# A four-layer residual block: the last stores of First move to ScalarE's queue, and attention's first mask and gathers move one slot ahead

## The chip, the cores and the metric

The kernel runs on one core of one Trainium2 chip. A core has five engines with an instruction stream each: TensorE (PE), VectorE (DVE), ScalarE (ACT), GpSimd (POOL) and SyncE (SP). An engine works through its stream in order and waits on semaphores for the others. Transfers are issued from the streams of SP, ACT and POOL and are carried by 16 DMA engines. The metric is the device time of one execution in microseconds, as the median of several runs.

## The reference

`x` has 64 batches of 32 rows and 512 columns, in float32. Four layers are added to it in turn. All indices (which weight, which adapter, which pages, how long the cache is) are inputs.

```
x = x + L0(x)    W = weights[cond]                     (64, 32, 32);  einsum('bct,bcd->bdt', x, W)
x = x + L1(x)    x @ base.T + bias + (x @ A[id].T) @ B[id].T          adapters of rank 16
x = x + L2(x)    attention over a paged cache, 32 heads of queries, 8 of keys, D = 128:
                   q, k, v = x @ Wq.T, x @ Wk.T, x @ Wv.T
                   q, k = rope(rmsnorm(q)), rope(rmsnorm(k))          positions from cache_seqlens
                   keys = [k_cache[block_table] (512 rows), k (32 rows)], values alike
                   scores = q . keys / sqrt(D), cache rows >= cache_seqlens set to -1e30
                   out = (softmax(scores) . values) @ Wo.T
x = x + L3(x)    as L0, with other weights
```

## The kernel before, in words

The 2048 rows of x are 16 tiles of 128 rows (`NT`), four batches each. The kernel has two parts: one long scheduled part with L0, L1 and the attention of L2, and a last one with the product by Wo and L3.

**First** (class `First`, line 389) is L0 and L1 for one tile t: `load`, `fetch` (gathers of weights), `turn_x` and `keep_x` (PE multiplies x by the mix matrix so that it comes out turned, ACT copies it out of PSUM as `x1T`), `ranks` (PE, `h_ps`, from `x1T`), `linear` (PE, `l_ps`), `add` (DVE, writes the new x), `store_x`, `turn_out` (PE turns the new x), `keep_out` (ACT copies it out as `x2T`, the tile x_a or x_b), `store` (writes the turned rows to `xT_dram`), and for every second tile `sums` (DVE makes four half-tiles of sums and differences of a pair of tiles, in two tiles) and `store_sums` (writes these two tiles to `xS_dram`). The projections of attention read `xT_dram` and `xS_dram` later. `queue` (line 516) says who issues the three kinds of stores: SP up to tile 12, POOL for tiles 13, 14 and 15.

**Projections** (`Block`, `Norm`) run two tiles at a time, spread over 32 slots. A norm has `squares` (ACT, L720, four of them), `power` (POOL, L725 and L727: it makes `rstd`), and four pieces on DVE: `scale` (L732, needs `rstd`), `straight` (L739), `swapped` (L751) and `sum` (L761). `norm_piece` takes these four from one list, in order, as slots have room. Then PE turns the result (`turn`, L766) and ACT copies it out (`keep`, L778).

**Attention** (`Unit`, line 783) is one batch and half of the key heads: 128 units, each with four slots. A unit loads its keys by SP (`kT`, L804), gathers its values by POOL (`fetch_values`, L105, four gathers), makes its mask on POOL (`mask`, L819, tile `pen`), and in slot k of its four does the scores (PE, L848 and L851, into the one buffer `s_ps`), the masked reduction on DVE (L856, reads `pen` and frees `s_ps`) and the exponential on ACT (L867). Two slots later PE turns the probabilities (L890), three slots later it multiplies them by the values (L900).

**The order** is written out by hand. Time is counted in slots: 0 to 511 are the slots of attention, and negative ones come before it. `at(slot, where, do, ...)` puts a call on a plan, and `slot(i)` (line 1218) runs the plan of slot i in a fixed order: "fetch", "pool", then scores, values and turns of attention, then "out", "pe", "take", "late", "power", a norm piece, "turn", "dve", two norm pieces, "keep", "act", "store". The order in which calls are made is the order in each engine's stream. First's tile t has its home slot at -39 + 2t (line 1077): its `store_x` is in slot home + 3, `store` in home + 4 and `store_sums` in home + 5, all in "store"; `keep_out` is in home + 3 and `keep_x` in home, both in "keep"; `sums` is in home + 4, "power". So tile 15 (home -9) does `keep_x` in slot -9, `keep_out` and `store_x` in -6, `store` and `sums` in -5, and `store_sums` in -4; tile 13 (home -13) does `sums` in slot -9. The last norms before attention have their power steps in slots -5, -3 and -2. Their pieces on DVE follow: `scale` and `straight` of the norm with the power step of slot -3 are in slot -1, ahead of slot 0's masked reduction.

**Memory.** The tiles of First are in the pool `first`. When slot -2 begins, that pool is closed (line 1314), and the pools of attention (`pages`, `v`, `attn`, and `ps_o` in PSUM) are opened in the memory that it leaves. The first tile of a new pool waits for the last uses of the old one. The first unit's mask and its first two gathers are in "pool" of slot -2, its other two gathers in "pool" of slot -1.

Of the kernel before, what the change touches and what calls it, by code (L numbers as in the profile page):

```python
# [45 lines left out]
NT = B * S // P  # L46
# [6 lines left out]
KG = HK // NG  # L53
# [24 lines left out]
def resid_kernel(  # L78
# [19 lines left out]
    nc = tc.nc  # L98
# [109 lines left out]
    xT_dram = [dram.tile([P, NC, P], F32, name=f"xT_{t}") for t in range(NT)]  # L208

    xS_dram = [dram.tile([P, 2, NC, P], F32, name=f"xS_{p}") for p in range(NT // 2)]  # L210
# [16 lines left out]
    with ExitStack() as l2:  # L227
# [161 lines left out]
        class First:  # L389
# [123 lines left out]
                if p == 0:  # L513
                    pair_of[0].x["12"], pair_of[0].x["34"] = s, r

            def queue(self):

                return nc.sync if self.t < NT - 3 else nc.gpsimd

            def store_x(self):  # L520
                self.queue().dma_start(out=x_dram[self.t], in_=self.x)

            def store(self):
                self.queue().dma_start(out=xT_dram[self.t], in_=self.x2T)

            def store_sums(self):
                for i in (0, 1):
                    self.queue().dma_start(out=xS_dram[self.t // 2][:, i], in_=self.s[i])

        lora = {}  # L530
        last_scores = []
# [418 lines left out]
        def at(slot, where, do, *args):  # L950
            plan.setdefault((slot, where), []).append((do, args))
# [5 lines left out]
        step_of, pair_of, unit_of, turn_of, first_of = {}, {}, {}, {}, {}  # L957
# [118 lines left out]
        for t in range(NT):  # L1076
            home = -WINDOW - AHEAD - 6 + 2 * t
            f = [first_of, t]
            if t:
                at(home - 5 if t > 1 else begin, "fetch", make, *f, First, t)  # L1080
                at(home - 4 if t > 1 else begin + 1, "fetch", call, *f, "load")
            at(max(begin, home - 4) if t > 1 else begin, "pool", call, *f, "fetch")
            if t % 2 == 0:
                at(home - 3 if t else begin, "pool", call, *f, "fetch_a")
                if t == 0:
                    at(begin, "pool", call, *f, "fetch_b")
            at(home - 1, "power", call, *f, "diagonal")
            if t:
                for name in "ax"[t % 2 :]:
                    at(home, "turn", call, *f, f"turn_{name}")  # L1090
                    at(home, "keep", call, *f, f"keep_{name}")
                at(home + 1, "late", call, *f, "ranks")
                at(home + 1, "late", call, *f, "linear", (0, 1, 2))
            else:

                at(home, "turn", call, *f, "turn_x")
                at(home, "keep", call, *f, "keep_x")
                at(home, "act", call, turn_of, -1, "turn")
                at(home, "act", call, *f, "linear", (0, 1, 2, 3))
                at(home, "act", call, turn_of, -1, "keep")  # L1100
                at(home, "act", call, *f, "turn_a")
                at(home, "act", call, *f, "keep_a")
                at(home + 1, "late", call, *f, "ranks")
            at(home + 1, "power", call, *f, "own_ranks")
            at(home + 2, "pe", call, *f, "linear", (3, 4) if t else (4,))
            at(home + 2, "power", call, *f, "add")
            at(home + 3, "store", call, *f, "store_x")
            at(home + 3, "turn", call, *f, "turn_out")
            at(home + 3, "keep", call, *f, "keep_out")
            at(home + 4, "store", call, *f, "store")  # L1110
            if t % 2:
                at(home + 4, "power", call, *f, "sums")
                at(home + 5, "store", call, *f, "store_sums")

            home = SLOTS * t + 9
            turning.add(home)
            at(home - 6, "fetch", lambda t: make(turn_of, t, Turn, 1, t, room["pages"], 1), t)
            at(home, "turn", call, turn_of, t, "turn")
            at(home, "keep", call, turn_of, t, "keep")
            at(home + 1, "store", call, turn_of, t, "store")  # L1120
# [14 lines left out]
                at(-27 + c, "store", store_angles, c)  # L1135
        for u in range(len(units)):
            at(KG * (u - 1) if u > 1 else (ready, -1)[u], "fetch", make, unit_of, u, Unit, u)
            at(KG * (u - 1) + 1 if u else -2, "pool", call, unit_of, u, "mask")
            for c in range(NC):
                at(KG * u - 2 + c if u else -2 + c // 2, "pool", call, unit_of, u, "fetch_values")  # L1140
            at(u // NB * SLOTS + 4 + 3 * (u % NB), "fetch", call, unit_of, u, "fetch_new")
            at(KG * u - 2, "act", call, unit_of, u, "begin")

# [46 lines left out]
        home = n - 33  # L1190
# [72 lines left out]
        with tc.manual_schedule(engines=ENGINES):  # L1263

            lora["base"] = first_pool.tile([P, NC, HID], F32, name="base_sb")
            make(first_of, 0, First, 0)
            first_of[0].load()
            with_identity()
            adapt_sb = first_pool.tile([P, NT // 2], I32, name="adapt_sb")
            for i in (0, 1):  # L1270
                nc.sync.dma_start(
                    out=adapt_sb[i * P // 2 : (i + 1) * P // 2, :],
                    in_=bass.AP(
                        tensor=ints.tensor,
                        offset=ints.offset + I_ADAPT + i,
                        ap=[[2 * N_INT, P // 2], [2, NT // 2]],
                    ),
                )
            for half in (lo, hi):
                nc.sync.dma_start(out=lora["base"][:, half, :], in_=base_w[:, half, :])  # L1280
            lora["rows"] = rows_of(first_pool, "lora_rows", adapt_sb, NT // 2, RANK, lane16_f)

            lora["bias"] = first_pool.tile([P, HID], F32, name="bias_sb")
            slot(begin)
            more = angles()
            next(more)
            nc.gpsimd.dma_start(out=lora["bias"], in_=across(base_b, HID))
            for i in range(begin + 3, begin + 15):
                for _ in range(1 + (begin + 5 < i < begin + 11)):
                    at(i, "store", next, more, None)  # L1290
            for j in (0, 1):
                at(begin + 4, "store", load_kv_weights, 0, 1, j)
                at(begin + 5, "store", load_kv_weights, 0, 0, j)
            for c in range(2 * KG):
                at(begin + 8 + c, "store", load_q_weights, 0, c // 2, c % 2)
            for i in range(begin + 1, begin + 11):
                slot(i)
                if i == begin + 2:
                    for c in range(NC):
                        base_chunk(c)  # L1300
                    lora["mask"] = [own_ranks(0), own_ranks(1)]
                    nc.sync.dma_start(out=table, in_=ints[:, I_TABLE:])
                if i == begin + 8:
                    nc.vector.tensor_copy(seq_f, ints_sb[:, I_SEQ : I_SEQ + B])
                    key_i = wpool.tile([P, LA], I32, name="key_i", tag="w9")
                    nc.gpsimd.iota(key_i, pattern=[[1, LA]], base=0, channel_multiplier=0)
                    nc.vector.tensor_copy(key_f, key_i)
                    nc.vector.memset(key_f[:, L:], -BIG)
                    v_rows = rows_of(const, "v_rows", table, B * NC, PSIZE, lane32_f)
            for i in range(begin + 11, n + VLAG):  # L1310
                if i == ready - 1:
                    start.close()
                    room["kT"] = l2.enter_context(tc.tile_pool(name="kT", bufs=2))
                if i == -2:
                    first.close()
                    pages = ExitStack()
                    room["pages"] = pages.enter_context(
                        tc.tile_pool(name="pages", bufs=1, side="right")
                    )
                    room["v"] = l2.enter_context(tc.tile_pool(name="v", bufs=2))  # L1320
                    room["attn"] = l2.enter_context(tc.tile_pool(name="attn", bufs=2))
                    room["o"] = l2.enter_context(tc.tile_pool(name="ps_o", bufs=1, space=PSUM))
                if i == SLOTS * NT + 8:
                    pages.close()
                if i == n - 27:
                    assert not pieces
                    proj.close()
                    o_pools.append(
                        ctx.enter_context(tc.tile_pool(name="o_first", bufs=1, side="right"))
                    )  # L1330
                slot(i)
            run(n + VLAG, "store")
# [205 lines left out]
```

## Time and profile before

| | us |
|---|---|
| median of 3 runs | 2435.49 |
| lowest and highest run | 2434.86, 2442.51 |
| the profiled execution | 2438.05 |
| its span, from the first instruction to the last | 2436.2 |
| PE busy between 200 and 250 us | 50.00 of 50.00 |
| PE busy between 166 and 172 us | 4.94 of 6.00 |
| PE busy between 174.0 and 178.9 us | 2.46 of 4.90 |
| mean TensorE clock granted over the span | 0.999 |
| mean clock between 179.9 and 181.5 us | 0.55 |
| mean clock between 181.5 and 183.5 us | 0.51 |

Times inside the profile count from the start of the span. In a row of the timeline the first number is the start, the second the duration, then come engine, line, operation, the tiles written and read, and in brackets the idle time of the engine before the row and what ended it. In the waits, a row gives the engine and line that waited, what it waited for, the total, the number of times and the longest. In the table of stretches, the columns after the stretch's own length are the busy times of PE, PE's weight loads, DVE, ACT and POOL with their counts of instructions, then the granted clock, the share of the DMA engines and GB/s. Slot 0 begins at 174.5 us, with the first scores.

### The profile page before, as it was taken

Reading aid. Unit: us, or ns where it says so; the run is one execution under the profiler, and the core shown is the slowest. Engines: PE = TensorE matmul, PEld = TensorE weight load, DVE = VectorE, ACT = ScalarE, POOL = GpSimd, SP = SyncE. Lnnn points to the kernel's source line nnn. Section 1 sums busy time; section 2 is a strip of 40 time slices with the busy share of each in tenths; the row PEclk is TensorE's granted clock in tenths of the full one; section 3 lists DMA queues with packets and bytes.
Section 4 is the critical chain, followed back from the end, with each engine's and each line's share of the span. In section 5 each row is a group of like instructions: output and inputs, shape, how many; then the busy total and the mean of one; then the engine's idle time right before and its main releaser. Section 6 shows DMA issues by size and latency. Waiting matters only on the chain.

```text
span 2436.2 us, 47122 instructions
## 1 busy us (share of the span) xinstructions
PE 2401.7 (99%) x13792; PEld 1865.9 (77%) x13792; DVE 1651.7 (68%) x3555; ACT 1401.0 (58%) x4006; POOL 1231.2 (51%) x1269
## 2 busy tenths in 40 slices
PE   8999999999999999999999999999999999999999
PEld 4657777777777777777777777777777788888887
DVE  6557777777777777787777777777787756333222
ACT  2346777777777777777777777767677763000000
POOL 4336665566565657665665666665556653000000
PEclk9999999999999999999999999999999999999999
DMA  8876666676666677766666666666667874333221
GB/s 277 258 240 181 196 191 205 184 207 184 204 184 203 191 213 242 231 187 189 179 185 176 190 176 184 180 186 182 180 181 226 251 250 143 107 119 122 87 90 59
DMA packets 461055, 452.09 MB, mean 186 GB/s; under 512 B 67728, under 2 KB 383760, under 8 KB 457216
## 3 DMA queue, kind: packets, MB, share of 16 engines
q1 hardware_dynamic: 404960, 269.05, 36.7%
q0 software_dynamic: 55024, 179.25, 24.7%
q8 instruction: 111, 1.82, 0.3%
q14 instruction: 144, 1.18, 0.2%
q10 hardware_dynamic: 816, 0.79, 0.1%
HBM read 380.73 MB, written 76.55 MB: 188 GB/s over the span
## 4 chain that ended last, share of the span: by engine, by line
PE 92%; DMA 3%; ACT 1%; DVE 1%; SPq 1%; issue 1%; POOL 0%; ACTq 0%; DVEq 0%; POOLq 0%
PE proj_ps L664 23%; PE o_ps L900 17%; PE out_ps L1362 15%; PE s_ps L848 10%; PE pT_ps L890 9%; PE s_ps L851 9%; PE head_ps L766 3%; PE l_ps L481 2%; PE o_ps L913 1%; DMA kT<-kT 1%; DMA o<-oT 1%; PE s_ps L883 1%; SPq L804 1%; PE mix_ps L1380 1%; PE x1T_ps L450 1%
## 5 line engine op out<-in xcount | busy, mean ns | idle before, releaser
L105 POOL DMA_INDIRECT v_sb<-v,v_rows x512 | 544.2, 1063 | 361.7 <-PE o_ps L900 248.3
L900 PE MATMUL o_ps<-pT,v_sb 128*128 128x128 f32 x4096 | 624.5, 275 | 2.9 <-DVE pT L892 2.6
L900 PEld LDWEIGHTS o_ps<-pT,v_sb 128*128 128x128 f32 x4096 | 578.0, 191 | 31.0 <-DVE pT L892 3.9
L867 ACT ACTIVATE sm<-sm,top 128x544 f32<-128x544 f32 x512 | 380.8, 744 | 335.2 <-DVE top L856 245.5
L856 DVE CUSTOM_DVE_ANT_0 sm<-s_ps,pen 128x544 f32<-128x544 f32 x512 | 369.3, 721 | 112.7 <-PE s_ps L851 97.1
L873 ACT ACTIVATE sm<-sm,share 128x512 f32<-128x512 f32 x512 | 369.8, 722 | 105.3 <-DVE share L872 68.5
L892 DVE COPY pT<-pT_ps 128x512 f32<-128x512 f32 x512 | 353.2, 690 | 60.2 <-PE pT_ps L890 12.5
L848 PE MATMUL s_ps<-kT,qT 128*128 128x288 f32 x1024 | 335.0, 409 | 3.3 <-DVE top L856 2.4
L890 PE MATMUL pT_ps<-ident,sm 128*128 128x128 f32 x2048 | 309.9, 274 | 4.3 <-ACT qT L778 3.7
L676 DVE TENSOR_TENSOR raw<-proj_ps,raw 128x512 f32<-128x512 f32 x332 | 224.3, 688 | 132.2 <-PE proj_ps L664 115.9
L851 PE MATMUL s_ps<-kT,qT 128*128 128x256 f32 x1024 | 304.8, 379 | 2.0 <-DMA kT<-kT 1.0
L848 PEld LDWEIGHTS s_ps<-kT,qT 128*128 128x128 f32 x1024 | 179.5, 191 | 151.0 <-issue 128.3
L819 POOL TENSOR_SCALAR pen<-key_f,seq_f 128x544 f32<-128x544 f32 x128 | 283.2, 2212 | 13.2 <-DMA kT<-kT 1.9
L890 PEld LDWEIGHTS pT_ps<-ident,sm 128*128 128x128 f32 x2048 | 239.1, 142 | 8.3 <-ACT qT L778 4.8
L720 ACT ACTIVATE sq<-raw 128x128 f32<-128x128 f32 x640 | 198.4, 310 | 73.9 <-DVE raw L676 56.0
L851 PEld LDWEIGHTS s_ps<-kT,qT 128*128 128x128 f32 x1024 | 194.6, 190 | 56.5 <-issue 1.4
L105 POOL DMA_INDIRECT mix_rows<-in_w,cond_rows x32 | 37.3, 1165 | 344.2 <-DVE mix_diag L170 299.8
L872 DVE RECIPROCAL share<-total 128x1 f32<-128x1 f32 x512 | 83.9, 164 | 180.4 <-ACT sm L867 153.1
L725 POOL TENSOR_SCALAR ss<-ss 128x4 f32<-128x4 f32 x160 | 38.6, 241 | 308.7 <-ACT sq L720 303.0
L1412 ACT COPY p<-out_ps 128x256 f32<-128x256 f32 x7 | 2.6, 372 | 333.1 <-PE out_ps L1362 333.1
L664 PE MATMUL proj_ps<-sum,x 128*128 128x512 f32 x380 | 188.0, 597 | 0.0
L727 POOL TENSOR_TENSOR rstd<-ss,minus_half 128x4 f32<-128x4 f32 x160 | 169.8, 1061 | 13.4
(175 smaller groups left out, 3573.7 us busy)
## 6 DMA issues: line engine op xcount, KB each, us to landing
kT<-kT SPq DMA_DIRECT2D x2048, 64.0 KB
o_in<-o SPq DMA_DIRECT2D x28, 1024.0 KB
o<-oT POOLq DMA_DIRECT2D x69, 256.0 KB
o<-oT SPq DMA_DIRECT2D x58, 256.0 KB
v<-in_kv_cache SPq DMA_DIRECT2D x32, 256.0 KB
kT<-page_rows SPq DMA_DIRECT2D x32, 256.0 KB
vn<-raw SPq DMA_DIRECT2D x32, 256.0 KB
v_sb<-v,v_rows POOLq DMA_INDIRECT x512
```

The lines of the kernel that those rows point to most:

```text
L105: nc.gpsimd.indirect_dma_start(out=dst, out_offset=None, in_=table, in_offset=bass.IndirectOffsetOnAxis(ap=index, axis=0),)
L664: nc.tensor.matmul(self.ps, lhsT=self.pair.x[x][:, c if x == "b" else half.start + c, :], rhs=blocks(self.b)[w][:, c, :], start=(c == 0), ...
L819: nc.gpsimd.tensor_scalar(self.pen, key_f, seq_f[:, self.b : self.b + 1], BIG, ALU.is_ge, ALU.mult)
L848: nc.tensor.matmul(ps[:, first:HID], lhsT=q, rhs=self.kT[:, :n1, k, :], start=True, stop=True)
L851: nc.tensor.matmul(ps[:, HID : first + LA], lhsT=q, rhs=self.kT[:, n1:, k, :], start=True, stop=True)
L856: nc.vector.tensor_tensor_reduce(out=sm, in0=ps[:, first : first + LA], in1=self.pen, scale=1.0, scalar=3e38, op0=ALU.add, op1=ALU.min, ac ...
L867: nc.scalar.activation(sm, sm, AF.Exp, bias=top, scale=-1.0, accum_out=total)
L873: nc.scalar.activation(sm[:, :L], sm[:, :L], AF.Copy, scale=share)
L890: nc.tensor.transpose(ps[:, c, :], self.sm[k][:, c * P : (c + 1) * P], ident)
L892: nc.vector.tensor_copy(pT, ps)
L900: nc.tensor.matmul(o_of[self.s, k][:, self.j, :], lhsT=self.v[c][:, k * D : (k + 1) * D], rhs=self.pT[k][:, c, :], start=(self.j == 0 and ...
L1362: nc.tensor.matmul(ps[:, :HALF], lhsT=o[:, i, :], rhs=w[i // REP][:, i % REP, :], start=(i == 0), stop=(i == KG * REP - 1),)
```

## The change

For tiles 13, 14 and 15, `store` and `store_sums` are issued by ACT instead of POOL; `store_x` stays on POOL. `store` of these tiles moves from "store" of slot home + 4 to "keep" of slot home + 3, right behind `keep_out`, and `store_sums` of tiles 13 and 15 from "store" of slot home + 5 to "turn" of slot home + 4, which comes after the DVE sums of the same slot. The pool `first` is closed and attention's pools are opened at slot -3 instead of -2; the first unit's mask and first two gathers are in "pool" of slot -3, the other two gathers in "pool" of slot -2.

```diff
-            def queue(self):
-
-                return nc.sync if self.t < NT - 3 else nc.gpsimd
+            def queue(self, last=nc.gpsimd):
+
+                return nc.sync if self.t < NT - 3 else last
 
             def store_x(self):
                 self.queue().dma_start(out=x_dram[self.t], in_=self.x)
 
             def store(self):
-                self.queue().dma_start(out=xT_dram[self.t], in_=self.x2T)
+                self.queue(nc.scalar).dma_start(out=xT_dram[self.t], in_=self.x2T)
 
             def store_sums(self):
                 for i in (0, 1):
-                    self.queue().dma_start(out=xS_dram[self.t // 2][:, i], in_=self.s[i])
+                    self.queue(nc.scalar).dma_start(out=xS_dram[self.t // 2][:, i], in_=self.s[i])
...
             at(home + 3, "store", call, *f, "store_x")
             at(home + 3, "turn", call, *f, "turn_out")
             at(home + 3, "keep", call, *f, "keep_out")
-            at(home + 4, "store", call, *f, "store")
+            at(home + 3 if t > NT - 4 else home + 4, "keep" if t > NT - 4 else "store", call, *f, "store")
             if t % 2:
                 at(home + 4, "power", call, *f, "sums")
-                at(home + 5, "store", call, *f, "store_sums")
+                if t > NT - 4:
+                    at(home + 4, "turn", call, *f, "store_sums")
+                else:
+                    at(home + 5, "store", call, *f, "store_sums")
...
-            at(KG * (u - 1) + 1 if u else -2, "pool", call, unit_of, u, "mask")
+            at(KG * (u - 1) + 1 if u else -3, "pool", call, unit_of, u, "mask")
             for c in range(NC):
-                at(KG * u - 2 + c if u else -2 + c // 2, "pool", call, unit_of, u, "fetch_values")
+                at(KG * u - 2 + c if u else -3 + c // 2, "pool", call, unit_of, u, "fetch_values")
...
-                if i == -2:
+                if i == -3:
                     first.close()
                     pages = ExitStack()
```

## The prediction

> **What bounds the kernel now.** I first read the busy times of the page, then PE's busy time by stretches of 50 us, then whom PE waited for.
>
> ```profile
> PE 2401.7 (99%) x13792; PEld 1865.9 (77%) x13792; DVE 1651.7 (68%) x3555; ACT 1401.0 (58%) x4006; POOL 1231.2 (51%) x1269
> ...
> 150.00:200.00 50.00, 44.75 (x188) 27.13 (x187) 31.82 (x70) 25.68 (x76) 27.60 (x33) 0.97 0.69 209
> 200.00:250.00 50.00, 50.00 (x311) 38.76 (x310) 38.35 (x84) 36.93 (x109) 30.88 (x32) 1.00 0.63 175
> ...
> PE s_ps L848 <- DVE top L856: 2.4, 1, 2.4
> ```
>
> TensorE sets the time: 2401.7 of 2436.2 us, so whatever happens can win only from 34.5 us of idle time. The stretch 150 to 200 us, where First ends and attention begins, holds 5.25 us of it; the next one holds none. So an engine other than PE matters only where PE waits for it, and that is at slots -9 to 1, the place of this change. PE's longest wait there is 2.4 us at slot 1's scores, for DVE's reduction of slot 0's. The timeline of POOL, then that of DVE, shows what is behind it.
>
> ```profile
> 165.12 0.54 POOL L521 DMA_DIRECT2D x<-x_sb  x1 [2.74 <-DVE x_sb L429]
> 169.30 0.23 POOL L725 TENSOR_SCALAR ss<-ss 128x4 f32<-128x4 f32 x1 [3.65 <-ACT sq L720]
> 169.61 1.05 POOL L727 TENSOR_TENSOR rstd<-ss,minus_half 128x4 f32<-128x4 f32 x1
> 170.64 0.63 POOL L524 DMA_DIRECT2D xT<-x_b  x1
> 171.26 1.08 POOL L528 DMA_DIRECT2D xS<-x  x2
> 172.42 0.48 POOL L725 TENSOR_SCALAR ss<-ss 128x4 f32<-128x4 f32 x1
> 172.98 1.07 POOL L727 TENSOR_TENSOR rstd<-ss,minus_half 128x4 f32<-128x4 f32 x1
> 175.95 2.12 POOL L819 TENSOR_SCALAR pen<-key_f,seq_f 128x544 f32<-128x544 f32 x1 [1.90 <-DMA kT<-kT]
> 178.36 1.11 POOL L105 DMA_INDIRECT v_sb<-v,v_rows  x1 [0.28 <-issue]
> 179.77 0.96 POOL L105 DMA_INDIRECT v_sb<-v,v_rows  x1 [0.30 <-issue]
> 180.81 0.58 POOL L725 TENSOR_SCALAR ss<-ss 128x4 f32<-128x4 f32 x1
> 181.47 1.05 POOL L727 TENSOR_TENSOR rstd<-ss,minus_half 128x4 f32<-128x4 f32 x1
> ...
> 174.09 0.69 DVE L732 TENSOR_TENSOR raw<-raw,rstd 128x512 f32<-128x512 f32 x1 [0.21 <-POOL rstd L727]
> 174.81 0.69 DVE L739 TENSOR_TENSOR rot_a<-raw,rot_q 128x512 f32<-128x512 f32 x1
> 178.11 0.72 DVE L856 CUSTOM_DVE_ANT_0 sm<-s_ps,pen 128x544 f32<-128x544 f32 x1 [2.60 <-POOL pen L819]
> ```
>
> The mask (pen) is the first tile in memory that First has left, so it waits until the last use of that memory is over. The page names a kT load, but ACT's table load, held by the same pool, starts at 175.81, and the newest use is POOL's xS store, issued by 172.34. So I take the store's landing as the cause: 175.8 - 172.34 = 3.5 us. PE loses 2.42 us at 178.90, and its clock falls right after (0.55 from 179.9 to 181.5, 0.51 to 183.5): 3.4 us at half speed, 1.7 us more. About 4.1 us is the most that the change could recover here, 0.17% of the time.
>
> **What the change does, part by part.** Seven issues leave POOL (three xT, four xS, 0.54 to 0.64 us each). POOL is idle around the first four, so that alone gains nothing.
>
> *(a) The seven issues on ACT.* The nearest row is ACT's three page_rows issues at 11.84: 2.65 us together, 0.435, 0.477 and 1.654. I take 0.45 each, and the spread for the range. What stands behind them on ACT decides. xT of t=13 follows its copy at 151.5; ACT has 2.09 us idle before 155.72, so it hides. xS of t=13 stands in "turn" of slot -9, in front of "keep", where ACT copies x1T of t=15; and it has to wait for DVE's sums:
>
> ```profile
> 155.72 0.59 ACT L460 COPY x1T<-x1T_ps 128x512 f32<-128x512 f32 x1 [2.09 <-PE x1T_ps L450]
> ...
> 156.56 0.42 DVE L511 TENSOR_TENSOR x<-x_a,x 128x256 f32<-128x256 f32 x1
> ...
> 156.38 1.14 PE L465 MATMUL h_ps<-x1T,aT 128*128 128x128 f32 x8
> ```
>
> The sums end at 156.98; the second issue adds 0.5, so the copy starts at 157.5 instead of 155.72. PE's h_ps waits for that copy, and behind h_ps stands all of PE: **+1.8 us** (0 if ACT gets past the waiting store, 3.0 with an issue of 1.65). PE, DVE and ACT all move by this. xT of t=14 sits in 2.43 us of ACT idle. It may also wait for an earlier transfer, as a kT load (about 2 us to land) comes before it in the program; ACT's next copy comes at 163.97, so that is hidden too. xT and xS of t=15 fall where ACT is dense, between the copies and the squares: I add 0.25 us before the first squares and 0.6 before the next. The first leaves rstd ready 0.2 us before DVE wants it; the second ends in ACT's copy L684, at 176.4, while PE wants it at 177.2. Both cost nothing; with issues of 1.65 they would cost about 1 us.
>
> *(b) The mask.* The last xS issue moves to ACT, and by its place there: old squares end 169.21, +1.8 of shift, +0.25, but the issue need not wait for the last square; the two issues end at 171.85. How long such a store takes to land on this queue no row shows. The bounds are the chain of waits' 2.04 us for a 64 KB kT load at 173.93 and its 6.86 us for a 256 KB kT store at 142.75; POOL's 3.5 us is the nearest. I take 3.0: pen starts at 174.9, **1.05 us earlier** than now (173.9 to 178.7 by the bounds).
>
> The page "DMA: Bandwidth & Descriptors" of the Trainium skill (Issuing engines are not separate DMA queues) speaks against the idea of the change: every queue runs on the same 16 engines, so moving a store saves only issue time. The 3.5 us above fits that. By its fixed 2.0 us plus bytes over 436 GB/s, an estimate of 2.6 us, the sum below would be 0.4 us smaller.
>
> *(c) What is now queued behind the mask.* In a slot, "pool" runs before "power". With the mask and two gathers at slot -3, they stand in front of slot -3's power step, the pair at 172.42 and 172.98, which used to run during the wait. Its rstd is what DVE's L732 waits for at 174.09 (0.21 us already now), and L732 and L739 stand in DVE's order ahead of slot 0's reduction. So the power step, not the mask, ends last. From pen's start to the end of the power step behind two gathers the rows above show 182.52 - 175.95 = 6.57 us. Then L732 and L739: from 174.09 to 175.50, 1.41 us, and 0.07 for the two handovers. The reduction starts at 174.9 + 8.05 = 182.95 instead of 178.11: **+4.85 us in all**, which holds the +1.8 of (a) and the -1.05 of (b); alone, (c) is worth 4.1. For this to be a gain without (a), pen would have to start before 170.06, while POOL is busy with the step before until 170.66.
>
> *(d) Gathers.* The third and fourth leave POOL at about 183.6, before PE reaches slot 3, now 4.85 us later. PE's 0.26 us wait at 189.17 goes: **-0.26**. The moved power step of slot -2 is then done at 185.3, and DVE asks for it at 187.8: nothing. SP's kT loads of the second unit may wait up to 2.5 us for ACT's stores; they are wanted at slot 4, past 190: nothing.
>
> *(e) Clock.* PE's hole at slot 1 grows from 2.42 to about 5.5 us; half speed after it is the row 0.55/0.51 now, 1.7 us, and up to twice that if the phase is bad: I take **+0.4**. The hole of (a), 1.8 us, is shorter than the one that brought the drop: 0, at most +1.7. The skill's page "TensorE: Matmul & The Clock Gate" (Part 1) has windows of 3.4 us that run freely, as long as the drop here. By that rule the price turns on where the hole falls in a window.
>
> Everything after slot 1 is PE without holes, so nothing takes this up again. **Sum:** 4.85 - 0.26 + 0.4 = +5.0. The profiled execution took 2438.05 (span 2436.2 and 1.85 around it), so 2443.0 for it; it lies 2.56 above the median of 2435.49, so **2440.5** as a median. With pen at 173.9 it is +4.0; if (a) and the landing are both at their least, pen starts at 172.4 and the sum is +2.0; with the longest landing it is +8.8.
>
> **Rivals.**
> *It works as named (faster).* If slot 0's reduction is not held by rstd, PE's 2.42 us and the 1.7 us of half clock go: 2435.5 - 4.1 = 2431.4. The point is the power step of slot -3: it must end by about 176.6 on the old time scale. For it: the mask does come sooner. Against it: the three rows between pen's start and rstd need 6.57 us. 0.08.
> *Half of it.* ACT slips past the waiting xS store, or the copy L460 is not what PE waits for; then (a) is nothing, the landing is early, and +2.0 to +3.0 is left: 2438. For it: ACT's issue at 11.84 ran beside a copy. Against it: the next copy there waited until 14.59. 0.14.
> *Worse.* The xS store lands after 5.9 us, as the kT store at 149.69, and both holes bring the clock down: 4.85 + 2.9 - 0.26 + 0.4 + 1.7 = +9.6, 2445.1. For it: DMA share is 0.92 from 172 to 174. Against it: POOL's store there took 3.5. 0.14.
>
> **How the numbers follow.** The forecast has 0.64 and its own range is 2438 to 2444. The range for 8 in 10 is 2434 to 2445: it takes in the half case, leaves out most of the faster one and the upper half of the worse one. A measurement here can tell about 0.3% from no change, 7.3 us, so faster means below 2428.2 and slower above 2442.8. No case is faster by that much: 0.02 for what I have not seen. Slower gets the worse case and the upper end of the forecast: 0.16. Within 0.3%: 0.82.
>
> **What would show it.** In the changed profile h_ps at slot -8 has about 1.8 us of PE idle before it, put down to ACT's x1T. POOL has pen, two gathers, then L725 and L727, and pen starts 1 us earlier. DVE's L732 waits some 6 us for rstd, and slot 1's scores come near 183.7. I am wrong if pen is still what DVE's first L856 waits for, if h_ps has no hole, or if slot 1's scores start before 178.9.

## The result and the profile after

| | before | after |
|---|---|---|
| median, us (6 runs each) | 2436.74 | 2452.22 |
| lowest and highest run | 2434.86, 2442.51 | 2445.97, 2455.02 |
| the profiled execution | 2438.05 | 2455.02 |
| its span | 2436.2 | 2453.3 |
| mean TensorE clock granted over the span | 0.999 | 0.996 |

The changed kernel is slower: ratio 1.0057, 95% interval [1.0044, 1.007]; that is 15.5 us by the medians and 13.9 us by the ratio. A second measurement, told below under "Both once more", gave 1.0038 [1.0024, 1.0051], 9.0 us. The forecast of 2440.5 and its range up to 2445 were too low.

First the busy line of the changed kernel's page, then its busy time by stretches (columns as before: PE, weight loads, DVE, ACT, POOL, granted clock, DMA share, GB/s).

```profile
PE 2405.3 (98%) x13792; PEld 1867.0 (76%) x13792; DVE 1651.4 (67%) x3555; ACT 1401.5 (57%) x4006; POOL 1227.8 (50%) x1262
```

```profile
150.00:200.00 50.00, 33.52 (x105) 18.26 (x104) 21.81 (x46) 16.66 (x52) 16.22 (x17) 0.83 0.58 181
200.00:250.00 50.00, 50.00 (x283) 38.31 (x282) 38.35 (x85) 33.34 (x93) 33.24 (x34) 1.00 0.64 184
...
162.00:166.40 4.40, 0.00 (x0) 0.00 (x0) 0.00 (x0) 0.59 (x1) 0.00 (x0) 0.51 0.52 164
166.40:172.40 6.00, 5.98 (x13) 3.56 (x14) 2.18 (x4) 0.00 (x0) 0.00 (x0) 0.51 0.38 112
192.70:199.60 6.90, 4.92 (x11) 3.28 (x12) 5.01 (x13) 3.39 (x8) 6.06 (x6) 0.51 0.31 86
```

The loss is in the stretch where it was looked for: between 150 and 200 us PE is busy 33.52 us instead of 44.75, and the next stretch is full in both kernels. Two pieces ran at half clock, 162.0 to 172.4 and 192.7 to 199.6; in the first, PE did nothing for 4.4 us and then worked 6 us at half speed. PE's waits say whom it waited for:

```profile
PE h_ps L465 <- ACT x1T L460: 9.2, 2, 8.9
PE s_ps L848 <- DVE top L856: 5.7, 1, 5.7
```

The two places are those of the prediction. The second is as large as forecast, the first five times as large. ACT's timeline shows why:

```profile
156.47 0.35 ACTq L524 DMA_DIRECT2D xT<-x_b  x1
156.86 0.59 ACT L778 COPY qT<-head_ps 128x512 f32<-128x512 f32 x1 [4.38 <-PE x1T_ps L450]
159.94 5.80 ACTq L528 DMA_DIRECT2D xS<-x  x2
165.78 0.59 ACT L460 COPY x1T<-x1T_ps 128x512 f32<-128x512 f32 x1 [6.74 <-DMA kT<-kT]
```

```profile
156.46 1.02 PE L664 MATMUL s_ps<-sum,x 128*128 128x512 f32 x2
166.42 2.08 PE L465 MATMUL h_ps<-x1T,aT 128*128 128x128 f32 x8 [8.94 <-ACT x1T L460]
...
187.03 0.71 PE L848 MATMUL s_ps<-kT,qT 128*128 128x288 f32 x2
...
194.68 1.33 PE L848 MATMUL s_ps<-kT,qT 128*128 128x288 f32 x2 [5.66 <-DVE top L856]
```

Tile 13's two xS stores stretch over 5.80 us on ACT: the row runs from the first issue at 159.94 to the end of the second at 165.74, with a wait between them. Only then comes the x1T copy that h_ps waits for. The bracket does not name the sums on DVE, for which I had let the stores wait, but a key load (kT), a transfer of SP. SP issued the first unit's sixteen key loads from 158.81 to 169.08, around that wait:

```profile
158.81 10.27 SPq L804 DMA_DIRECT2D kT<-kT  x16
```

Behind the hole, h_ps takes 2.08 us instead of 1.14 and the matmuls after it 4.74 instead of 2.84: half clock, which puts another 2.5 us between h_ps (10.04 us later than before) and the next x2T_ps (12.54 later). The second hole, in the timelines of POOL and DVE:

```profile
181.94 0.23 POOL L725 TENSOR_SCALAR ss<-ss 128x4 f32<-128x4 f32 x1 [3.72 <-ACT sq L720]
182.25 1.05 POOL L727 TENSOR_TENSOR rstd<-ss,minus_half 128x4 f32<-128x4 f32 x1
185.91 2.50 POOL L819 TENSOR_SCALAR pen<-key_f,seq_f 128x544 f32<-128x544 f32 x1 [2.62 <-DMA kT<-kT]
188.69 1.11 POOL L105 DMA_INDIRECT v_sb<-v,v_rows  x1 [0.28 <-issue]
190.10 0.96 POOL L105 DMA_INDIRECT v_sb<-v,v_rows  x1 [0.30 <-issue]
191.14 0.23 POOL L725 TENSOR_SCALAR ss<-ss 128x4 f32<-128x4 f32 x1
191.45 1.04 POOL L727 TENSOR_TENSOR rstd<-ss,minus_half 128x4 f32<-128x4 f32 x1
```

```profile
192.53 0.69 DVE L732 TENSOR_TENSOR raw<-raw,rstd 128x512 f32<-128x512 f32 x1 [6.12 <-POOL rstd L727]
193.26 0.69 DVE L739 TENSOR_TENSOR rot_a<-raw,rot_q 128x512 f32<-128x512 f32 x1
193.90 0.72 DVE L856 CUSTOM_DVE_ANT_0 sm<-s_ps,pen 128x544 f32<-128x544 f32 x1
```

Mask, two gathers, then the power step; DVE waits 6.12 us for rstd in front of the reduction that frees `s_ps`. This is step (c) row by row.

### The profile page after: what moved, and what is told of

Same layout as the page of the kernel before. It is cut to its first block, busy times and chain, and to the rows that moved or that the text cites. A ratio compares the mean times of both kernels' runs of the same rounds, so it can differ in the third digit from the quotient of the medians.

```text
span 2453.3 us, 47120 instructions
## 1 busy us (share of the span) xinstructions
PE 2405.3 (98%) x13792; PEld 1867.0 (76%) x13792; DVE 1651.4 (67%) x3555; ACT 1401.5 (57%) x4006; POOL 1227.8 (50%) x1262
## 3 DMA queue, kind: packets, MB, share of 16 engines
q8 instruction: 111, 1.82, 0.3%
## 4 chain that ended last, share of the span: by engine, by line
PE 93%; DMA 2%; DVE 1%; ACT 1%; issue 1%; SPq 1%; POOL 0%; ACTq 0%; DVEq 0%; POOLq 0%
PE proj_ps L664 23%; PE o_ps L900 18%; PE out_ps L1365 15%; PE s_ps L848 10%; PE pT_ps L890 9%; PE s_ps L851 9%; PE head_ps L766 3%; PE l_ps L481 3%; PE o_ps L913 1%; DMA kT<-kT 1%; PE s_ps L883 1%; PE h_ps L465 1%; PE mix_ps L1383 1%; PE x1T_ps L450 1%; SPq L804 1%
## 5 line engine op out<-in xcount | busy, mean ns | idle before, releaser
L856 DVE CUSTOM_DVE_ANT_0 sm<-s_ps,pen 128x544 f32<-128x544 f32 x512 | 369.0, 721 | 111.0 <-PE s_ps L851 98.2
L890 PE MATMUL pT_ps<-ident,sm 128*128 128x128 f32 x2048 | 309.6, 274 | 3.6 <-ACT qT L778 2.7
L819 POOL TENSOR_SCALAR pen<-key_f,seq_f 128x544 f32<-128x544 f32 x128 | 284.0, 2218 | 13.9 <-DMA kT<-kT 2.6
L890 PEld LDWEIGHTS pT_ps<-ident,sm 128*128 128x128 f32 x2048 | 238.9, 142 | 7.3 <-ACT qT L778 3.7
L664 PE MATMUL proj_ps<-sum,x 128*128 128x512 f32 x380 | 188.0, 597 | 0.0
```

The lines of the kernel that those rows point to most:

```text
L664: nc.tensor.matmul(self.ps, lhsT=self.pair.x[x][:, c if x == "b" else half.start + c, :], rhs=blocks(self.b)[w][:, c, :], start=(c == 0), ...
L819: nc.gpsimd.tensor_scalar(self.pen, key_f, seq_f[:, self.b : self.b + 1], BIG, ALU.is_ge, ALU.mult)
L856: nc.vector.tensor_tensor_reduce(out=sm, in0=ps[:, first : first + LA], in1=self.pen, scale=1.0, scalar=3e38, op0=ALU.add, op1=ALU.min, ac ...
L890: nc.tensor.transpose(ps[:, c, :], self.sm[k][:, c * P : (c + 1) * P], ident)
```

## The experiments

Times are medians; each run was compared with runs of before on its own chip, and those differed between chips (2432.5, 2432.8 and 2436.9), so the differences count, not the absolute times. The diffs are against the changed kernel unless said otherwise.

**The stores alone**

```diff
-            at(KG * (u - 1) + 1 if u else -3, "pool", call, unit_of, u, "mask")
+            at(KG * (u - 1) + 1 if u else -2, "pool", call, unit_of, u, "mask")
...
-                at(KG * u - 2 + c if u else -3 + c // 2, "pool", call, unit_of, u, "fetch_values")
+                at(KG * u - 2 + c if u else -2 + c // 2, "pool", call, unit_of, u, "fetch_values")
...
-                if i == -3:
+                if i == -2:
```

> The seven stores stay on ACT; the pool close, the mask and the gathers are back at slot -2 as before. Theory of two holes (ACT's waiting xS store of tile 13 makes the long hole at h_ps; the mask and two gathers ahead of the power step make the smaller one at slot 1): the h_ps hole stays at 7 to 10 us, put down to ACT x1T, with lowered clock near it; slot 1's scores wait less than 1 us for DVE's reduction; median 2443 to 2449 against 2436.7 before. Rival, the slot move is the whole cause: about 2437, no hole at h_ps above 1 us. Rival, the stores on ACT alone are the whole cause: as slow as after, about 2452.

2438.89 against 2432.52: +6.4 us, 1.0027 [1.0016, 1.0037]. PE's timeline of this run:

```profile
165.04 2.07 PE L465 MATMUL h_ps<-x1T,aT 128*128 128x128 f32 x8 [7.99 <-ACT x1T L460]
...
187.33 0.75 PE L848 MATMUL s_ps<-kT,qT 128*128 128x288 f32 x2 [0.81 <-DVE top L856]
```

The hole at h_ps is 7.99 us, the one at slot 1 fell to 0.81 (2.42 before). So ACT's stores alone make the long hole. They also do what the change is named for: POOL went from the power step to the mask without a wait, and slot 1's hole shrank by 1.6 us.

**The slot alone**

```diff
-                self.queue(nc.scalar).dma_start(out=xT_dram[self.t], in_=self.x2T)
+                self.queue().dma_start(out=xT_dram[self.t], in_=self.x2T)
...
-                    self.queue(nc.scalar).dma_start(out=xS_dram[self.t // 2][:, i], in_=self.s[i])
+                    self.queue().dma_start(out=xS_dram[self.t // 2][:, i], in_=self.s[i])
...
-            at(home + 3 if t > NT - 4 else home + 4, "keep" if t > NT - 4 else "store", call, *f, "store")
+            at(home + 4, "store", call, *f, "store")
...
-                if t > NT - 4:
-                    at(home + 4, "turn", call, *f, "store_sums")
-                else:
-                    at(home + 5, "store", call, *f, "store_sums")
+                at(home + 5, "store", call, *f, "store_sums")
```

> The stores are POOL's again at their old slots; only the pool close, the mask and the gathers stand at slot -3. Theory of two holes: no hole at h_ps; pen starts no earlier than before (about 176, since the memory is given free by the same store), and the power step of slot -3 is behind it, so slot 1's scores wait about 8 us instead of 2.4, with up to 2 us of lowered clock; median 2441 to 2446. Rival, ACT's stores are the whole cause: 2437 or less and a hole at slot 1 of no more than 2.4 us.

2437.93 against 2432.52: +5.4 us, 1.0018 [1.0009, 1.0028]. In this stretch PE has no wait for x1T, but one of 8.42 us at slot 1; the mask started at 176.07, no earlier than before. POOL's timeline of this run, then PE's:

```profile
176.07 2.12 POOL L819 TENSOR_SCALAR pen<-key_f,seq_f 128x544 f32<-128x544 f32 x1 [4.20 <-DMA kT<-kT]
...
184.41 1.33 PE L848 MATMUL s_ps<-kT,qT 128*128 128x288 f32 x2 [8.42 <-DVE top L856]
```

As expected, neither part alone is the whole loss.

**Tile 13's sums back on POOL**

```diff
-                    self.queue(nc.scalar).dma_start(out=xS_dram[self.t // 2][:, i], in_=self.s[i])
+                    self.queue(nc.scalar if self.t > NT - 2 else nc.gpsimd).dma_start(out=xS_dram[self.t // 2][:, i], in_=self.s[i])
...
-                if t > NT - 4:
+                if t > NT - 2:
                     at(home + 4, "turn", call, *f, "store_sums")
```

> As after, but the two xS stores of tile 13 are POOL's again, at their old slot; the turned rows of tiles 13 and 14 stay on ACT. Theory that the two xS stores in front of the x1T copy make the long hole: the h_ps hole falls from 8.9 us to below 2; slot 1's hole stays at 3 to 6 us; median 2438 to 2445. Rival, any store on ACT in this stretch waits as long for an earlier transfer of SP (the turned rows then hold the copy): the hole stays at 5 us or more, and the time at 2447 or more.

2438.62 against 2432.52: +6.1 us, 1.0021 [1.001, 1.0031]. In this stretch no wait for x1T is left; slot 1's hole is 5.49 us. Of seven stores, two make the long hole.

**The mask behind the power step**

```diff
-            at(KG * (u - 1) + 1 if u else -3, "pool", call, unit_of, u, "mask")
+            at(KG * (u - 1) + 1 if u else -3, "pool" if u else "turn", call, unit_of, u, "mask")
...
-                at(KG * u - 2 + c if u else -3 + c // 2, "pool", call, unit_of, u, "fetch_values")
+                at(KG * u - 2 + c if u else -3 + c // 2, "pool" if u or c > 1 else "turn", call, unit_of, u, "fetch_values")
```

> As after, but in slots -3 the mask and the first two gathers come behind the power step instead of in front of it; the other two gathers stay in slot -2. Theory: the h_ps hole stays at 7 to 10 us; the 5.7 us at slot 1's scores fall below 1.5 us; the time is 3 to 6 us less than after, 2446 to 2449. Rival, slot 1's scores wait because the mask itself is late: the hole at slot 1 stays above 4 us and the time within 2 us of after.

2441.71 against 2432.52: +9.2 us, 1.0033 [1.0019, 1.0047]. The h_ps hole stayed (8.10), slot 1's fell to 0.81. But the other two gathers of slot -2 stand in front of that slot's power step, and the wait came back there: DVE's next L732, for the norm of slot -2, waited 1.82 us for rstd, and PE 1.37 us at L890 and 1.00 us at L664 behind it. How much this run gains on the changed kernel can't be read from medians of different chips; by the table below, the shift at slot 64 is 9.8 us instead of 14.0.

**The key loads later.** This run was to settle what the store waits for.

```diff
-        ready = -8
+        ready = -6
```

> As after, but the sixteen key loads (kT) of the first unit are issued two slots later, at slot -6. Theory: the xS store of tile 13 waits on ACT for the landing of SP's key loads, not for its own sums, so with the loads issued later that wait goes and only what I had priced is left: the h_ps hole falls from 8.9 us to 1 to 3 us, and the row that names kT in front of ACT's x1T copy is gone. Rival, the store waits for its place in busy DMA engines or costs ACT that long by itself: the hole stays at 6 us or more. The total isn't what the run is for: the keys of slot 0 now land late, which may cost 2 to 6 us of PE at slot 0.

2435.47 against 2432.84: +2.6 us, 1.0017 [1.0008, 1.0026]. ACT's timeline of this run, then PE's:

```profile
157.03 0.99 ACTq L528 DMA_DIRECT2D xS<-x  x2
158.07 0.58 ACT L460 COPY x1T<-x1T_ps 128x512 f32<-128x512 f32 x1 [2.30 <-DVE x L511]
```

```profile
158.71 1.16 PE L465 MATMUL h_ps<-x1T,aT 128*128 128x128 f32 x8 [1.48 <-ACT x1T L460]
```

With nothing about the stores changed, only the key loads moved, the two stores take 0.99 us instead of 5.80, the wait before the copy is put down to DVE's sums, and the hole is 1.48 us. The late keys cost PE 0.85 and 0.54 us at slot 0, less than I had allowed for. Moving the loads also takes traffic away, so this run alone doesn't rule out that the stores waited for a place in the DMA engines. The DMA shares do: in this run the engines are busy throughout from 155 to 159 us (share 1.05 by the profile's account) and the stores go out at once; in the changed kernel the share is 0.61 from 157 to 162 us and 0.50 from 163 to 165.3 us, while the second store waits. What that store waited for stands in the changed kernel's chain of work that ended last (start, duration, piece):

```profile
162.42 2.92 DMA kT<-kT
165.41 0.33 ACTq L528
165.78 0.59 ACT x1T L460
166.42 2.08 PE h_ps L465 x8
```

The store goes out 0.07 us after a key load has landed. How one engine's transfer comes to wait for another's can be read in the built program, and the semaphore times in the trace agree with it. All transfers of SP and ACT take eight completion semaphores in turn, in one order merged from both engines, and each first waits until the transfer eight places ahead has landed. POOL's transfers have eight semaphores of their own. In the merged order four of the key loads stand ahead of tile 13's turned rows, though the kernel makes the calls for the loads two slots later. Then tile 13's turned rows wait for tile 12's (landed at 156.39), the first xS store for those turned rows (159.86), the second for the sixth key load (165.34). With the loads at slot -6 the same stores stand ahead of all of them.

**The stores behind the copy**

```diff
-                    at(home + 4, "turn", call, *f, "store_sums")
+                    at(home + 4, "turn" if t > NT - 2 else "act", call, *f, "store_sums")
```

> As after, but ACT's two xS stores of tile 13 stand behind its x1T copy of tile 15 instead of in front of it. Theory that the wait costs only through what is queued behind it: the stores wait as long as in after (5 us or more on ACT), but the h_ps hole is below 0.5 us, and since ACT's next copy comes about 4 us later than the x1T copy, at most 2 us of the hole comes back there; slot 1's hole stays at 5 to 6 us; 7 to 11 us less than after, about 4 to 7 us above before. Rival, PE is held by the transfers themselves or by ACT as a whole: 5 us or more of PE idle stay between slots -9 and -5.

2437.73 against 2432.84: +4.9 us, 1.0018 [1.0008, 1.0027]. ACT's timeline:

```profile
155.02 0.35 ACTq L524 DMA_DIRECT2D xT<-x_b  x1
...
157.51 0.57 ACT L460 COPY x1T<-x1T_ps 128x512 f32<-128x512 f32 x1
157.83 5.10 ACTq L528 DMA_DIRECT2D xS<-x  x2
162.97 0.58 ACT L497 COPY x_a<-x2T_ps 128x512 f32<-128x512 f32 x1 [4.89 <-DMA kT<-kT]
```

and PE's:

```profile
158.13 1.16 PE L465 MATMUL h_ps<-x1T,aT 128*128 128x128 f32 x8 [2.01 <-ACT x1T L460]
```

The stores hold ACT as long as ever, 5.10 us, but now the copy of x_a stands behind them, ahead of which ACT had 4.65 us of idle time in the kernel before; PE lost nothing there. So the price is what is queued behind the wait. The hole at h_ps is 2.01 us, not below 0.5 as expected: the turned rows of tile 13 wait too (the copy ahead of them ended at 151.12, they went out at 155.02), and behind them four squares and the x1T copy. How long they wait differs between runs: with tile 13's sums on POOL they went out 1.7 us after their copy and cost PE nothing.

**Tile 15 on SP.** Before, with the stores of tile 15 alone on the queue that has nothing urgent behind them:

```diff
-                self.queue().dma_start(out=xT_dram[self.t], in_=self.x2T)
+                self.queue(nc.sync if self.t > NT - 2 else nc.gpsimd).dma_start(out=xT_dram[self.t], in_=self.x2T)
...
-                    self.queue().dma_start(out=xS_dram[self.t // 2][:, i], in_=self.s[i])
+                    self.queue(nc.sync if self.t > NT - 2 else nc.gpsimd).dma_start(out=xS_dram[self.t // 2][:, i], in_=self.s[i])
...
-                at(home + 5, "store", call, *f, "store_sums")
+                at(home + 5 if t < NT - 1 else home + 4, "store", call, *f, "store_sums")
```

(`queue` takes the argument as in the changed kernel.)

> Before, with one change: the turned rows and the xS stores of tile 15 are issued by SP (in slot -5) instead of POOL; nothing is on ACT, and attention's pools stand at slot -2 as before. SP has only key loads of the second unit behind them, which are wanted 15 us later. Theory that the mask waits for the last store's landing and that a queue with nothing urgent behind it is the place for it: pen starts about 174.2 instead of 175.95, right behind the power step of slot -3; slot 1's hole falls from 2.4 us to below 1; the lowered clock behind it is gone; 2 to 4 us faster than before. Rival, the mask waits for a key load or something else of the memory's owner: pen stays near 176, the time within 1 us of before.

2431.51 against 2432.84: 0.9993 [0.9984, 1.0002]. POOL's timeline, then PE's:

```profile
172.91 2.91 POOL L819 TENSOR_SCALAR pen<-key_f,seq_f 128x544 f32<-128x544 f32 x1
```

```profile
176.64 0.75 PE L848 MATMUL s_ps<-kT,qT 128*128 128x288 f32 x2 [0.73 <-DVE top L856]
...
182.29 0.63 PE L890 MATMUL pT_ps<-ident,sm 128*128 128x128 f32 x4 [1.37 <-issue]
...
187.56 0.49 PE L900 MATMUL o_ps<-pT,v_sb 128*128 128x128 f32 x2 [0.90 <-DMA v_sb<-v,v_rows]
```

The mask starts without a wait, the hole is 0.73 us and no clock drop follows. So it was the last store's landing that held the mask; in the profile of before it landed at 175.36 by the semaphore times, ahead of the mask at 175.95, and in the built program the mask waits for that store and for no key load. The gain, 1.3 us by the medians, is smaller than expected and not clear of noise: PE waits 1.37 and 0.90 us soon after, where before it worked at half clock.

**Only tiles 14 and 15 on ACT, old slot.** The kernel of "tile 13's sums back on POOL" with the three edits of "the stores alone" (the turned rows of tile 13 stay on ACT too).

> As after without its two holes: the xS stores of tile 13 are POOL's again and the pool close, mask and gathers are at slot -2; the turned rows of tiles 13 to 15 and the xS stores of tile 15 are on ACT. Theory: no hole at h_ps; the xS stores of tile 15 hold ACT some 2 us and with it the squares and the power step of slot -3, so pen starts near 175.5, the hole at slot 1 is 1.5 to 2.5 us; within 2 us of before. Rival, stores on ACT free the mask as meant: pen at 174.5 or sooner, hole below 1 us, 2 to 4 us faster than before.

2435.05 against 2432.84: 1.0009 [1.0, 1.0019]. The mask started at 175.08 and slot 1's hole was 1.79 us: a little better there than before, as the first theory had it, and no gain in the time.

**Both once more**

> The changed kernel once more, beside the experiments' chip. Theory that the two parts add: the stores alone were 6.4 us and the slot alone 5.4 us above before by medians, and in their profiles the shift of the 64th slot was 8.4 and 5.1 us; so 11 to 15 us above before, with a hole of 8 to 9 us at h_ps and one of 5 to 6 us at slot 1. Rival, the first measurement was a draw with slow transfers: 8 us or less above before, an h_ps hole under 6 us.

2445.85 against 2436.85: +9.0 us, 1.0038 [1.0024, 1.0051]. The holes are 8.04 and 5.58 us, as expected; the time rose less than expected.

> The version with only tile 15's turned rows and sums on SP once more, for its interval. The slot-1 hole (0.7 instead of 2.4 us) makes it 1.7 us faster; the lowered clock it also avoids was hidden, since slots 1 to 3 kept the same distance from slot 0 in both. So 1 to 2.5 us faster than before. Rival, no difference: within 0.5 us.

2434.39 against 2436.85: 0.9991 [0.9982, 1.0], 2.5 us faster and within what was expected, though the interval reaches no change.

The table sets the profiles beside each other. "Shift" is how much later than in the profile of before slot 64's reduction (L856) starts, less the offset that was there already ahead of the edits (h_ps's start without its hole, or, where it has none, PE's L664 that is at 171.21 in before).

| run | h_ps hole | slot 1 hole | shift at slot 64 | slots 448 to 511 take |
|---|---|---|---|---|
| before | 0 | 2.42 | 0 | 222.7 |
| after | 8.94 | 5.66 | 14.0 | 223.0 |
| after, again | 8.04 | 5.58 | 13.6 | 217.7 |
| stores alone | 7.99 | 0.81 | 7.7 | 215.7 |
| slot alone | 0 | 8.42 | 5.6 | 216.9 |
| tile 13's sums on POOL | 0 | 5.49 | 3.0 | 221.0 |
| mask behind power | 8.10 | 0.81 | 9.8 | 221.2 |
| key loads later | 1.48 | 2.48 | 3.7 | 217.0 |
| stores behind the copy | 2.01 | 6.01 | 5.6 | 217.6 |
| tile 15 on SP | 0 | 0.73 | -0.8 | 218.0 |
| tile 15 on SP, again | 0 | 0.73 | -1.8 | 221.0 |
| tiles 14 and 15, old slot | 0 | 1.79 | -0.5 | 216.0 |

Two things are read from it. The parts add: 7.7 + 5.6 = 13.3, beside 13.6 and 14.0 for the whole. And the last column, in which no edit lies, varies by 7.3 us from one execution to the next. That is more than any difference between a shift and its run's difference of medians. It may also be why one kernel was measured 15.5 and 9.0 us slower, two results whose intervals overlap (10.7 to 17 and 5.8 to 12.4 us); that it is the reason is not shown. Both profiles of the first comparison, of before and after, happen to have long ends. What varies there was not looked into.

## Why the prediction was wrong, step by step

*Step (a), the seven issues on ACT, failed.* I let tile 13's xS stores wait for DVE's sums alone and put +1.8 us at h_ps (0 to 3.0). The place, the copy behind them and PE behind the copy were right; the wait was another one. The hole is 8.94 us (8.04 the second time). I had written that the turned rows of tile 14 may wait for an earlier transfer, a key load, and dismissed it because their cover hides it; for the stores that have no cover I did not ask the same question. The order of the calls (these stores in slot -9, the key loads in slot -8) does not show the wait either; the merged order of the built program does. With the key loads moved away the hole was 1.48 us, so the working of the 1.8 was sound for the wait it knew. The turned rows of tile 13, which I had taken to hide in 2.09 us of idle time, waited as well and cost some 2 us by themselves in the run with the sums behind the copy, nothing in the one with the sums on POOL.

*The clock behind it (part of step e).* I gave the hole of (a) nothing, at most 1.7. Behind 8.94 us without work PE ran at half clock and lost 2.5 us. Together (a) measures 8.9 + 2.5 = 11.4 us instead of 1.8. These 9.6 us are the miss: in the profiles the whole change comes to 14.0 us at slot 64, where the sum gave 5.0, and the other terms together took 0.6 off.

*Steps (b) and (c), mask and power step, held.* The mask starts 2.59 us earlier against slot 0's scores, where 2.85 (1.05 and the 1.8 of (a)) was foretold. Slot 0's reduction was to come 3.05 us later besides (a) (4.85 - 1.8). It came 15.8 us later, slot 0's scores 12.55: 3.24. L732's wait is 6.12 us where "some 6" was foretold. The store's landing as what holds the mask was an inference; the mask without a wait in the run with tile 15 on SP bears it out. One lower bound does not follow from its terms: with (a) and the landing both at their least, pen starts at 170.05 + 2.04 = 172.1 and not at 172.4. That is 0.3 us and has no part in the miss.

*Step (d)* and the rest up to slot 64 gave back 0.7 us instead of 0.26 (15.8 at slot 0's reduction, 15.1 at slot 64's).

*Step (e) at slot 1* was to cost 0.4 and cost nothing, though the drop was twice as long as before. From slot 0's reduction to slot 64's it took 233.4 us in before with one drop behind slot 1, 232.7 in after with a drop twice as long, and 234.3 and 233.3 in the two profiles with tile 15 on SP and no drop. Four other runs with drops of 3.4 to 10.2 us around slot 1 took 232.8 to 233.2. So PE has slack there against the other engines; at half clock it works in what would be waits. The limit of this shows in "The mask behind the power step": there a later drop, at 194.84, came together with the new wait of 1.00 us, and the stretch took 235.7. For the same reason the 4.1 us that I took as the most that could be won were too many: the 2.42 us hole was real, the 1.7 us of clock were covered.

*The rivals.* "Worse" (2445.1) had its weight on a late landing and clock drops and came nearest. Its half about the clock came true, both holes brought it down; its late landing did not: the issue of the last xS store ended on ACT at 182.56, and the mask began 3.35 us later, at 185.91, where I had taken 3.0 and this rival 5.9. What made the first hole long was in no rival. "It works as named" was excluded by the power step, and the profile shows just that order.

## What to carry to other kernels

A transfer moved to another engine's stream comes under the waits of that stream's transfers, and they need not be its data's: look in the built program for every transfer, of any engine, that has to land first, and price the issue by the latest of them. Then ask what stands behind it on that engine; the same wait of 5 us, put behind the copy that PE needs and in front of one with idle time before it, took 6 us off a hole of 8. The better place for such a store was a queue with nothing urgent behind it, by the holes in the profiles; the gain in time was 1.3 and 2.5 us, at the edge of what the runs can tell. A price for lowered clock counted here only where PE itself set the pace behind the hole.

## What was not expected of the hardware

The clock stayed down for long after one hole: 10.2 us (162.1 to 172.3) with the 8.94 us hole, where it fell while PE was still idle, and 6.8 us with the 5.66 us one, beside 3.4 us in before with 2.42. Holes of nearly one length, 7.99, 8.10 and 8.04 us, came with drops of 6.8, 6.8 and 10.2 us, so the length of the hole does not settle it. Nor does it take one long hole: each drop in the twelve profiles begins at the end of 3.41 us in which PE was busy for 1.63 us or less, and with the key loads later these 3.41 us (1.39 us busy, up to 178.75) held only waits below 0.9 us. The Trainium skill's "TensorE: Matmul & The Clock Gate" (Part 1) has free-running windows of about 3.4 us; the three drops are three, two and one of these, which agrees. An issue on ACT with nothing to wait for took 0.33 to 0.36 us, less than the 0.45 I had taken from three issues early in the kernel. The end of attention, slots 448 to 511, took between 215.7 and 223.0 us in twelve profiles of kernels that are alike there.
